# A state-space and expert network on one core: planner durations replaced, and the scan of a unit split into four scans with given first states

## The chip, the cores and the metric

The kernel runs on one core of one Trainium2 chip, as one launch. The metric is the device time of an execution in microseconds; the median of the runs is compared. TensorE (PE), VectorE (DVE), ScalarE (ACT), GpSimd (POOL) and SyncE (SP, here the queue that issues transfers) run side by side, each through its own queue in order, and wait for each other on semaphores.

## The reference, cut to what matters

A picture x of 4 batches, 256 channels and 64 x 64 places is read as 4 sequences of 4096 tokens. Layer 0 is a selective state-space mixer (512 inner channels, 16 states a channel) between projections and gates. Layer 1 is a second state-space mixer with 8 heads, and then a feed-forward layer that sends every token to one of 8 experts. The change touches the recurrence of layer 0:

```python
def step(h, inp):
    dt_l, B_l, C_l, x_l = inp
    dA = jnp.exp(dt_l[..., None] * A)
    h = dA * h + (dt_l * x_l)[..., None] * B_l[:, None, :]
    y = jnp.einsum('bdn,bn->bd', h, C_l)
    return (h, y)
h0 = jnp.zeros((Bb, D_INNER, D_STATE), t.dtype)
_, ys = jax.lax.scan(step, h0, xs)
```

So for each batch, channel d and state n there is one first-order recurrence over 4096 tokens, which starts from zero. Its input is u B with u = dt x.

## The kernel before

**Stages.** `mixers` computes both mixers and the routing, `experts` the feed-forward layer in blocks of 256 tokens, `turn` the transposed output. Only `mixers` is touched.

**Chunks.** `mixers` goes through 64 chunks of T = 256 tokens, 16 for each batch. A chunk passes the steps front0, mid0, scan, tail0 and front1, and two chunks later ssd and back1, so that the steps of several chunks lie in flight together.

**Units of the scan.** In `scan`, a chunk's 512 channels with 16 states are 16 units (j, f), j over 4 blocks of channels, f over 4 sets of states. In a unit the 128 partitions hold 32 channels with 4 states each, and 4 groups q of such channels lie behind each other, 256 tokens each: tiles of 128 x 4 x 256. A unit has these operations:

- da = exp(dt A): 4 ScalarE activations, one for each q, with the column `neg_a0[:, j * SQ + q, f : f + 1]` as scale (dt4 is dt, spread over the partitions).
- ub = u4 * B: one VectorE product of 128 x 1024 into the PSUM tile `ub`, of which there is one.
- h: one VectorE `tensor_tensor_scan` over the 1024 elements as one line, from 0.0.
- hlast: a ScalarE copy of the last column of each group, the first state of the next chunk.
- p = h * C: a GpSimd product of 128 x 1024, then 8 TensorE matmuls that add p up into `py`.

Because one scan runs over four groups, a group's first decay has to be zero, or the state of the group ahead would run into it. The three da buffers (`decay_tile`) therefore get a zero in column 0 once, ahead of the stage, and the activations write columns 1 to 255. What the true first decay would bring, exp(dt A) at the first token times hlast of the chunk before, is computed apart as `e0` (once for each j: product on GpSimd, exponential on ScalarE, product on GpSimd) and added to column 0 of ub, the VectorE addition ub<-ub,e of 128 x 4. Chunks that begin a batch have no such correction: 60 chunks of 64 have it, that is 960 units of 1024.

**The order of the work.** Nothing in the stage is issued directly. `Plan` (r in the code) notes every operation with an engine, a duration, its operands and a slot, and `order` then plays it through: an event loop in which each free engine takes, of the operations that are ready and have room for their tiles, the one with the lowest slot. The order of the starts in this play is the order in which `issue` puts the instructions into the engines' queues (L378 is the line that issues, so all of them carry it in the profile). What enters:

- The durations come from formulas in `mm`, `transpose`, `act`, `copy`, `acts`, `dve`, `gps`, `dma` and `scatter`.
- `SIGNAL`, 0.15 us, is added between an operation and a user on another engine; on the same engine nothing is.
- `slot`: a chunk's number times 16, plus the step's place, plus a due-time shift from the table `SHIFT`, looked up by how many calls of `at` the chunk has made. For most calls of `scan` the shift is -2.2, for most others -0.3.
- `port`: GpSimd operations and VectorE operations with two operands in SBUF are not played at the same time. The scan, with ub in PSUM, is not such an operation.
- `ride`: p waits, up to `PATIENCE` = 4 us, until a scan has just begun, and gets a dependency on the VectorE instruction ahead of that scan, so that it runs beside the scan.

Of the kernel before, what the change touches and what calls it, by code (L numbers as in the profile page):

```python
# [20 lines left out]
P = 128  # L21
T = 256
# [24 lines left out]
SHIFT = {  # L47
    1: -2.3, 4: 1.4, 5: 0.2, 6: -1.3, 7: -0.3, 8: -0.3, 9: -0.3, 10: -0.3, 11: -0.3, 12: -0.3, 14: -0.3, 15: -0.3,
    16: -0.3, 17: -0.3, 18: -0.3, 19: -0.3, 20: -0.3, 21: -0.3, 22: -0.3, 23: -0.3, 24: -0.3, 25: -0.3, 26: -3.3,
    27: -2.2, 28: 0.2, 29: -0.1, 30: -2.2, 31: -2.2, 32: -2.2, 33: -2.2, 34: -2.2, 35: -2.2, 36: -2.2, 37: 1.2,  # L50
    38: 0.5, 39: -2.2, 40: -2.1, 41: -2.2, 42: -2.7, 43: -2.2, 44: -2.2, 45: -6.0, 46: -2.2, 47: -2.2, 48: -2.2,
    49: -2.2, 50: -2.2, 51: -2.2, 52: -9.4, 53: -2.2, 54: -1.4, 55: -2.2, 56: -2.2, 57: -2.2, 58: -2.2, 59: -2.2,
    60: -4.7, 61: -2.2, 62: -2.2, 63: -2.2, 64: -2.2, 65: -2.2, 66: -2.2, 67: -2.7, 68: -2.2, 69: -2.2, 70: -2.2,
    71: -0.1, 72: -2.2, 73: -2.2, 74: -2.2, 75: -5.9, 76: -4.8, 77: -2.2, 78: -2.2, 79: -2.7, 80: -2.2, 81: -2.2,
    82: -2.2, 83: -2.2, 84: -2.2, 85: -5.2, 86: -2.2, 87: -2.2, 88: -2.2, 89: -2.2, 90: -2.2, 91: -1.4, 92: -2.2,
    93: -2.2, 94: -2.2, 95: -2.7, 96: -2.2, 97: -2.2, 98: -2.2, 99: -2.2, 100: -2.2, 101: -2.2, 102: -2.2,
    103: -2.2, 104: -2.2, 105: -2.2, 106: -2.3, 107: -4.0, 108: -2.0, 109: -2.2, 110: -2.2, 111: -2.2, 112: -2.2,
    113: -1.8, 114: -1.3, 115: 0.9, 116: -0.3, 117: 1.8, 118: -0.3, 119: 0.1, 120: -0.3, 121: -0.3, 123: -0.3,
    124: -0.3, 125: -0.3, 126: 0.6, 127: -1.2, 128: -0.3, 129: -0.3, 130: 0.3, 131: 0.4, 132: -1.4, 133: -0.3,
    134: -0.3, 135: -0.3, 136: 1.6, 137: -0.3, 140: 0.6,  # L60
}
# [88 lines left out]
class Plan:  # L150
# [6 lines left out]
    SIGNAL = 0.15  # L157
# [61 lines left out]
    def mm(self, out, left, right, **kw):  # L219
        rows, n = out.shape[0], self.width(right)  # L220
        w = max(0.24, n / 550) if rows > 64 else max(0.16, n / 900) if rows > 32 else max(0.15, n / 1500)
        self.note("PE", w, self.nc.tensor.matmul, (out, left, right), kw, (out,), (left, right), join=out.root)

    def transpose(self, out, src, ident):
        w = 0.08 + 0.1 * src.shape[0] / P
        self.note("PE", w, self.nc.tensor.transpose, (out, src, ident), {}, (out,), (src,), join=out.root)

    def act(self, out, src, func, **kw):
        w = 0.2 + self.width(out) / 1200
        self.note("ACT", w, self.nc.scalar.activation, (out, src, func), kw, (out,), (src, *kw.values()))  # L230

    def copy(self, out, src):
        self.note("ACT", 0.2 + self.width(out) / 1200, self.nc.scalar.copy, (out, src), {}, (out,), (src,))
# [7 lines left out]
    def dve(self, name, *args, **kw):  # L241
        out, *rest = (*args, *kw.values())
        tensors = [a for a in rest if isinstance(a, Part) or hasattr(a, "ap")]
        n = max(self.width(a) for a in (out, *tensors))
        port = len([a for a in tensors if self.on_sbuf(a) and self.width(a) > 1]) > 1
        if name == "tensor_tensor_scan":
            n, port = 2 * n, False
        op = self.note("DVE", 0.14 + n / 960, getattr(self.nc.vector, name), args, kw, (out,), rest, port=port)
        op.scan = name == "tensor_tensor_scan"
        if op.scan:  # L250
            self.scans.append(op)

# [3 lines left out]
    def gps(self, name, *args, ride=False, **kw):  # L256
        w = 0.3 + self.width(args[0]) * 2.02e-3
        f = getattr(self.nc.gpsimd, name)
        self.note("POOL", w, f, args, kw, (args[0],), args[1:], port=True, ride=ride)
# [7 lines left out]
    def scatter(self, out, rows, src, bound):  # L267


        def f(out, rows, src):  # L270
            return self.nc.gpsimd.indirect_dma_start(
                out=out,
                out_offset=bass.IndirectOffsetOnAxis(ap=rows, axis=0),
                in_=src,
                in_offset=None,
                bounds_check=bound,
                oob_is_err=False,
            )

        self.note("POOL", 1.8, f, (out, rows, src), {}, (out,), (rows, src), lag=4.0)  # L280
# [3 lines left out]
    def order(self):  # L284
# [16 lines left out]
        for op in self.ops:  # L301
            if not op.missing:
                heappush(waiting[op.engine], (0.0, op.seq, op))
        done = 0
        scan = before = last = shared = None

        def room(op, now):
            for root in op.roots:
                if not root.begun:
                    ring, queue = rings.setdefault(root.ring, []), queues[root.ring]  # L310
                    ring[:] = [o for o in ring if o.left or o.until + self.SIGNAL > now]
# [6 lines left out]
        while done < len(self.ops):  # L318
# [6 lines left out]
            for e in engines:  # L325
# [3 lines left out]
                if free[e] > now:  # L329
                    continue  # L330
# [17 lines left out]
                heappush(events, free[e])  # L348
                if op.port:
                    port[e] = free[e]  # L350
# [7 lines left out]
                for root in op.roots:  # L358
                    root.left -= 1
                    root.until = max(root.until, op.end)  # L360
                    if not root.left:
                        heappush(events, root.until + self.SIGNAL)
                for u in op.users:
                    u.missing -= 1
                    late = op.end if u.engine == e and not op.lag else op.end + self.SIGNAL
# [23 lines left out]
def tile_conv_attn_hybrid(ctx: ExitStack, tc: tile.TileContext, a: dict, out: bass.AP, cap: int, st: int):  # L389
# [41 lines left out]
    def mixers(es):  # L431
# [220 lines left out]
        def silus(*tiles, gates=0):  # L652
# [5 lines left out]
            r.acts(sum(0.2 + Plan.width(t) / 1200 for t in tiles) / len(calls) + 2.6 / len(calls), calls)  # L658
# [162 lines left out]
        da_bufs = []  # L821
        for i in range(3):
            t = wp.tile([P, SQ, T], F32, name=f"da{i}", tag=f"da{i}")
            nc.gpsimd.memset(t[:, :, 0:1], 0.0)
            da_bufs.append(t)
        turn = iter(range(10**9))

        def decay_tile():
            return r.tile(lambda: da_bufs[next(turn) % len(da_bufs)], [P, SQ, T], "da", len(da_bufs))

        def scan(k_):
# [10 lines left out]
            for j in range(KD):  # L842
# [17 lines left out]
                k_.at(j * SQ - 1)  # L860
                if later:

                    e0 = work([P, SQ, SQ], "e0", 2)
                    r.gps("tensor_tensor", e0, neg_a0[:, sl], dt4[:, :, 0:1].to_broadcast([P, SQ, SQ]), ALU.mult)
                    r.act(e0, e0, AF.Exp)
                    r.gps("tensor_tensor", e0, e0, k_.prev.hlast[:, sl], ALU.mult)
                for f in range(SQ):
# [3 lines left out]
                    da = decay_tile()  # L871
                    for q in range(SQ):
                        r.act(da[:, q, 1:], dt4[:, q, 1:], AF.Exp, scale=neg_a0[:, j * SQ + q, f : f + 1])
# [3 lines left out]
                    if later:  # L877
                        r.tt(ub[:, :, 0], ub[:, :, 0], e0[:, :, f], ALU.add)
                    h = work([P, SQ, T], "h", 3)
                    r.dve("tensor_tensor_scan", h.flat(), da.flat(), ub.flat(), 0.0, ALU.mult, ALU.add)  # L880
# [652 lines left out]
```

## Time and profile before

| | us |
|---|---|
| median of 3 runs | 6952.74 |
| lowest, highest | 6948.43, 6954.37 |
| the profiled execution, its own time | 6966.12 |
| its span, first to last instruction | 6964.3 |
| first scan to last scan | about 110 to 5727 |
| experts | about 5727 to 6870 |
| output | about 6870 to 6964 |

The granted TensorE clock was 0.906 on average. In the profile's rows, out<-in names the tiles of the program; sizes are partitions x elements. A row of a group gives the busy time of all its instructions, the mean of one in ns, and the idle time of the engine just before them with what ended it. A row of the timeline gives start and duration in us. Durations of two instructions in a row on VectorE can overlap, since the next may start before the one ahead has left the pipeline; where this matters, the distance between two starts is the measure.

### The profile page before, as it was taken

The numbers are of one execution on the slowest core, as the hardware profiler recorded it, in microseconds if no ns is written. First come the engines' busy times: TensorE is split into PE (matmuls) and PEld (weight loads), VectorE is DVE, ScalarE is ACT, GpSimd is POOL, SyncE is SP. The second block draws the span as 40 slices with busy tenths as digits, with TensorE's granted clock in tenths as the row PEclk, the third lists the DMA queues.
The fourth block names the chain that finished last, engine by engine and source line by source line (L and its number), as shares of the span: only waits on it lengthen the run. The fifth ranks groups of instructions, "written<-read, shape, count | busy, mean of one in ns | idle before, by whom it ended". The sixth has DMA issues, their size and how long they took to land. (4 is left out here: it accounts for less than half of the span.)

```text
span 6964.3 us, 114017 instructions
## 1 busy us (share of the span) xinstructions
PE 6084.7 (87%) x37672; PEld 4128.5 (59%) x37672; DVE 5670.3 (81%) x7646; ACT 4892.5 (70%) x12007; POOL 3431.0 (49%) x2632
## 2 busy tenths in 40 slices
PE   5788888888888888888888888888888877999996
PEld 3455555555555555555555555555555546888886
DVE  4899999999999999999999999999999983434443
ACT  4778888888887778788887777878777863333332
POOL 3455555555555555555555555555555552333331
PEclk7899999999888988998898888989888888999998
DMA  6966667666666666666666666666666633555556
GB/s 178 255 172 178 181 178 182 178 178 178 178 177 173 174 172 176 174 176 171 174 178 177 175 178 176 179 177 176 171 175 176 174 106 132 189 194 197 193 191 238
DMA packets 1125137, 1245.56 MB, mean 179 GB/s; under 512 B 111888, under 2 KB 1093652, under 8 KB 1115330
## 3 DMA queue, kind: packets, MB, share of 16 engines
q1 hardware_dynamic: 1083458, 1008.76, 54.9%
q0 software_dynamic: 30000, 210.98, 8.5%
q10 hardware_dynamic: 11088, 18.53, 0.7%
q8 instruction: 299, 4.90, 0.3%
q14 instruction: 292, 2.39, 0.1%
HBM read 919.92 MB, written 311.63 MB: 177 GB/s over the span
## 5 line engine op out<-in xcount | busy, mean ns | idle before, releaser
L378 POOL TENSOR_TENSOR p<-h,bc 128x1024 f32<-128x1024 f32 x1024 | 2420.7, 2364 | 1980.3 <-DVE ub L378 1371.8
L378 DVE TENSOR_TENSOR_SCAN h<-da,ub 128x1024 f32<-128x1024 f32 x1024 | 2341.8, 2287 | 190.5 <-ACT da L378 69.1
L378 ACT ACTIVATE da<-dt,w_m_Alog 128x255 f32<-128x255 f32 x4096 | 1791.1, 500 | 26.1 <-DVE h L378 17.6
L378 DVE TENSOR_TENSOR ub<-u,bc 128x1024 f32<-128x1024 f32 x1024 | 1370.2, 1338 | 23.9 <-DMA dt<-dt_d 11.5
L378 PE MATMUL py<-p,sum 128*32 128x256 f32 x8192 | 719.0, 434 | 255.2 <-POOL p L378 242.9
L378 PE MATMUL b<-t,w_W_in 128*128 128x256 f32 x2304 | 640.2, 424 | 17.6 <-DVE res L378 10.5
L378 ACT COPY hlast<-h 128x4 f32<-128x4 f32 x1024 | 198.7, 194 | 598.7 <-DVE h L378 596.8
L378 PEld LDWEIGHTS py<-p,sum 128*32 128x32 f32 x8192 | 182.0, 114 | 693.9 <-POOL p L378 399.4
L378 PEld LDWEIGHTS b<-t,w_W_in 128*128 128x128 f32 x2304 | 458.7, 208 | 163.8 <-issue 44.2
L378 PE MATMUL a<-t,w_m_in_w 128*128 128x256 f32 x2048 | 549.8, 422 | 3.5 <-DVE t L378 3.5
L1381 PE MATMUL ph<-xt,w 128*128 128x256 f32 x2272 | 517.1, 381 | 11.5 <-DMA w<-in_w_exp_dram,w_at 6.4
L378 PEld LDWEIGHTS a<-t,w_m_in_w 128*128 128x128 f32 x2048 | 415.9, 211 | 149.5 <-issue 61.0
L1392 PE MATMUL po<-w,hid 128*128 128x256 f32 x2272 | 502.0, 379 | 0.0
L1381 PEld LDWEIGHTS ph<-xt,w 128*128 128x128 f32 x2272 | 427.3, 191 | 70.4 <-ACT hid L1383 7.3
L1392 PEld LDWEIGHTS po<-w,hid 128*128 128x128 f32 x2272 | 431.7, 190 | 58.7
L378 PE MATMUL a<-raw,taps_m 128*32 128x256 f32 x2048 | 211.3, 492 | 234.1 <-DMA raw<-raw_d 169.9
L378 PE MATMUL c<-cum,after 128*128 128x512 f32 x512 | 325.7, 724 | 96.8 <-DVE ex L378 89.9
L1358 DVE CAST number<-rows 128x2 uint32<-128x2 f32 x71 | 12.0, 170 | 476.1 <-DMA tok_d<-fixed,number 461.4
L1356 ACT ACTIVATE tn<-rows 128x256 f32<-128x256 f32 x142 | 82.5, 597 | 414.0 <-DMA rows<-buf_d,row_at 413.5
L1404 POOL DMA_INDIRECT tok_d<-fixed,number x142 | 145.9, 1028 | 390.0 <-DVE fixed L1402 307.6
L378 ACT ACTIVATE cum<-upto,da 128x128 f32<-128x128 f32 x1024 | 337.4, 396 | 0.0
L378 ACT ACT_TABLE_LOAD x256 | 328.4, 1283 | 4.5
(237 smaller groups left out, 11087.4 us busy)
## 6 DMA issues: line engine op xcount, KB each, us to landing
raw<-raw_d SPq DMA_DIRECT2D x2048, 128.0 KB
dt<-dt_d SPq DMA_DIRECT2D x1024, 128.0 KB
u<-u_d SPq DMA_DIRECT2D x1024, 128.0 KB
raw_d<-raw SPq DMA_DIRECT2D x128, 518.0 KB
gx_d<-pre SPq DMA_DIRECT2D x64, 1024.0 KB
bc<-bc_d SPq DMA_DIRECT2D x1024, 64.0 KB
gx<-gx_d SPq DMA_DIRECT2D x256, 256.0 KB
dt_d<-mid SPq DMA_DIRECT2D x64, 512.0 KB
```

What stands on the lines that cost most here:

```text
L378: op.issued = f(*map(placed, args), **{k: placed(v) for k, v in kw.items()})
L1356: act(tn[:, j], rows[:, j, TOK:], AF.Identity, scale=rows[:, j, 1:2], bias=rows[:, j, 2:3])
L1358: nc.vector.tensor_copy(number, rows[:, :, 3])
L1381: mm(ph, w1[:, k, f * P : (f + 1) * P], xt[:, k], start=k == 0, stop=k == KC - 1)
L1392: mm(po[:, j], hid[:, f, j * P : (j + 1) * P], w2[:, f], start=f == 0, stop=f == KF - 1)
L1404: nc.gpsimd.indirect_dma_start(out=tok_d, out_offset=bass.IndirectOffsetOnAxis(ap=number[:, j : j + 1], axis=0), in_=fixed[:, j], in_offse ...
```

## The change

It has two parts.

**The planner.** The table `SHIFT` is emptied, so every step has its plain slot. The durations of `mm`, `transpose`, `act`, `copy`, `acts`, `dve`, `gps` and `scatter` get new constants; an activation is charged 0.09 us more for each operand that is a column. `SIGNAL` becomes a value for each engine (0.12 to 0.21), and `BEHIND` is added between dependent operations of the same engine (0.13 for VectorE, 0.14 for ScalarE, 0.13 for GpSimd, none for TensorE). After a transfer 0.06 is added. In the play SP takes no further transfer while eight (`LANES`) are in flight.

**The scan.** A unit's scan becomes four of 256 elements, noted as one operation of the plan by the new `scans_of`, each with a first state: the column of the chunk before's hlast, or 0.0 in a chunk that begins a batch. The activations write all 256 columns of da, which becomes an ordinary tile with three buffers. The chain e0 (two GpSimd products and one exponential for each j), the addition to ub, the three da buffers and their memsets go.

```diff
--- before.py
+++ after.py
@@ -44,21 +44,7 @@
 TAIL, SSD, BACK = 18, 29, 37
 AHEAD = 4
 
-SHIFT = {
-    1: -2.3, 4: 1.4, 5: 0.2, 6: -1.3, 7: -0.3, 8: -0.3, 9: -0.3, 10: -0.3, 11: -0.3, 12: -0.3, 14: -0.3, 15: -0.3,
...
-}
+SHIFT = {}
 TOK = 4
 ROW = TOK + C
 
@@ -154,7 +140,9 @@
 
 
 
-    SIGNAL = 0.15
+    SIGNAL = {"DVE": 0.13, "ACT": 0.19, "PE": 0.21, "POOL": 0.12}
+    BEHIND = {"DVE": 0.13, "ACT": 0.14, "PE": 0.0, "POOL": 0.13}
+    LANES = 8
     SPARE = {}
     PATIENCE = 4.0
 
@@ -218,19 +206,20 @@
 
     def mm(self, out, left, right, **kw):
         rows, n = out.shape[0], self.width(right)
-        w = max(0.24, n / 550) if rows > 64 else max(0.16, n / 900) if rows > 32 else max(0.15, n / 1500)
+        w = max(0.224, n / 592) if rows > 64 else max(0.12, n / 1100) if rows > 32 else max(0.15, n / 1500)
         self.note("PE", w, self.nc.tensor.matmul, (out, left, right), kw, (out,), (left, right), join=out.root)
 
     def transpose(self, out, src, ident):
-        w = 0.08 + 0.1 * src.shape[0] / P
+        w = 0.11 if src.shape[0] > 64 else 0.2
         self.note("PE", w, self.nc.tensor.transpose, (out, src, ident), {}, (out,), (src,), join=out.root)
 
     def act(self, out, src, func, **kw):
-        w = 0.2 + self.width(out) / 1200
+        aps = sum(isinstance(v, Part) or hasattr(v, "ap") for v in kw.values())
+        w = 0.06 + self.width(out) / 1130 + 0.09 * aps
         self.note("ACT", w, self.nc.scalar.activation, (out, src, func), kw, (out,), (src, *kw.values()))
 
     def copy(self, out, src):
-        self.note("ACT", 0.2 + self.width(out) / 1200, self.nc.scalar.copy, (out, src), {}, (out,), (src,))
+        self.note("ACT", 0.05 + self.width(out) / 1200, self.nc.scalar.copy, (out, src), {}, (out,), (src,))
 
     def acts(self, weight, calls):
 
@@ -245,16 +234,26 @@
         port = len([a for a in tensors if self.on_sbuf(a) and self.width(a) > 1]) > 1
         if name == "tensor_tensor_scan":
             n, port = 2 * n, False
-        op = self.note("DVE", 0.14 + n / 960, getattr(self.nc.vector, name), args, kw, (out,), rest, port=port)
+        op = self.note("DVE", (0.06 if n > 4 else 0.14) + n / 960, getattr(self.nc.vector, name), args, kw, (out,), rest, port=port)
         op.scan = name == "tensor_tensor_scan"
         if op.scan:
             self.scans.append(op)
 
+    def scans_of(self, out, a, b, starts):
+
+        key, f = object(), self.nc.vector.tensor_tensor_scan
+        for i, start in enumerate(starts):
+            args = (out[:, i], a[:, i], b[:, i], start, ALU.mult, ALU.add)
+            w = 0.07 + self.width(out[:, i]) / 480
+            op = self.note("DVE", w, f, args, {}, (out[:, i],), (a[:, i], b[:, i], start), join=key)
+        op.scan = True
+        self.scans.append(op)
+
     def tt(self, out, a, b, op):
         self.dve("tensor_tensor", out, a, b, op)
 
     def gps(self, name, *args, ride=False, **kw):
-        w = 0.3 + self.width(args[0]) * 2.02e-3
+        w = 0.15 + self.width(args[0]) * 2.1e-3
         f = getattr(self.nc.gpsimd, name)
         self.note("POOL", w, f, args, kw, (args[0],), args[1:], port=True, ride=ride)
 
@@ -277,7 +276,7 @@
                 oob_is_err=False,
             )
 
-        self.note("POOL", 1.8, f, (out, rows, src), {}, (out,), (rows, src), lag=4.0)
+        self.note("POOL", 1.4, f, (out, rows, src), {}, (out,), (rows, src), lag=4.0)
 
 
 
@@ -301,6 +300,7 @@
         for op in self.ops:
             if not op.missing:
                 heappush(waiting[op.engine], (0.0, op.seq, op))
+        lanes, landings = ("SP",), []
         done = 0
         scan = before = last = shared = None
 
@@ -308,7 +308,7 @@
             for root in op.roots:
                 if not root.begun:
                     ring, queue = rings.setdefault(root.ring, []), queues[root.ring]
-                    ring[:] = [o for o in ring if o.left or o.until + self.SIGNAL > now]
+                    ring[:] = [o for o in ring if o.left or o.until > now]
                     while queue[-1].begun:
                         queue.pop()
                     if len(ring) + (queue[-1] is not root) * self.SPARE.get(root.ring, root.depth) >= root.depth:
@@ -326,7 +326,7 @@
                 while waiting[e] and waiting[e][0][0] <= now:
                     _, _, op = heappop(waiting[e])
                     insort(could[e], (op.slot, op.seq, op))
-                if free[e] > now:
+                if free[e] > now or e in lanes and len(landings) >= self.LANES and landings[-self.LANES] > now:
                     continue
                 for i, (_, _, op) in enumerate(could[e]):
 
@@ -346,6 +346,9 @@
                 op.start, op.end = now, now + op.weight + op.lag
                 free[e] = now + op.weight
                 heappush(events, free[e])
+                if e in lanes:
+                    landings.append(op.end)
+                    heappush(events, op.end)
                 if op.port:
                     port[e] = free[e]
                 if e == "DVE":
@@ -357,12 +360,12 @@
                     op.behind = before if scan and now - scan.start < 0.2 else shared
                 for root in op.roots:
                     root.left -= 1
-                    root.until = max(root.until, op.end)
+                    root.until = max(root.until, op.end + (0.06 if op.lag else self.SIGNAL[e]))
                     if not root.left:
-                        heappush(events, root.until + self.SIGNAL)
+                        heappush(events, root.until)
                 for u in op.users:
                     u.missing -= 1
-                    late = op.end if u.engine == e and not op.lag else op.end + self.SIGNAL
+                    late = op.end + (0.06 if op.lag else (self.BEHIND if u.engine == e else self.SIGNAL)[e])
                     u.ready = max(u.ready, late)
                     if u.ride and not u.missing:
                         heappush(events, u.ready + self.PATIENCE)
@@ -655,7 +658,7 @@
 
             calls += [(half_tanh, (t[:, :KC],), t[:, :KC], t[:, :KC]) for t in tiles[:gates]]
             calls.append((nc.scalar.preload_act_table_set, (SETS,), None, None))
-            r.acts(sum(0.2 + Plan.width(t) / 1200 for t in tiles) / len(calls) + 2.6 / len(calls), calls)
+            r.acts(sum(0.06 + Plan.width(t) / 1130 for t in tiles) / len(calls) + 2.6 / len(calls), calls)
 
         def inv_sqrt(dst, src, eps, scale=1.0):
 
@@ -818,16 +821,6 @@
 
 
 
-        da_bufs = []
-        for i in range(3):
-            t = wp.tile([P, SQ, T], F32, name=f"da{i}", tag=f"da{i}")
-            nc.gpsimd.memset(t[:, :, 0:1], 0.0)
-            da_bufs.append(t)
-        turn = iter(range(10**9))
-
-        def decay_tile():
-            return r.tile(lambda: da_bufs[next(turn) % len(da_bufs)], [P, SQ, T], "da", len(da_bufs))
-
         def scan(k_):
             later = k_.c > 0
             k_.hlast = work([P, NG, SQ], "hlast", 2)
@@ -857,27 +850,18 @@
                     for s in range(2):
                         r.dma("SP", gx[:, s], k_.gx_d[s * KD + j : s * KD + j + 2].rearrange("j p l -> p j l"))
                 sl = slice(j * SQ, (j + 1) * SQ)
-                k_.at(j * SQ - 1)
-                if later:
-
-                    e0 = work([P, SQ, SQ], "e0", 2)
-                    r.gps("tensor_tensor", e0, neg_a0[:, sl], dt4[:, :, 0:1].to_broadcast([P, SQ, SQ]), ALU.mult)
-                    r.act(e0, e0, AF.Exp)
-                    r.gps("tensor_tensor", e0, e0, k_.prev.hlast[:, sl], ALU.mult)
                 for f in range(SQ):
                     u = j * SQ + f
                     bc = bc4[f]
                     k_.at(u - 1)
-                    da = decay_tile()
+                    da = work([P, SQ, T], "da", 3)
                     for q in range(SQ):
-                        r.act(da[:, q, 1:], dt4[:, q, 1:], AF.Exp, scale=neg_a0[:, j * SQ + q, f : f + 1])
+                        r.act(da[:, q], dt4[:, q], AF.Exp, scale=neg_a0[:, j * SQ + q, f : f + 1])
                     k_.at(u)
                     ub = bank_u(SQ, T)
                     r.tt(ub, u4, bc[:, 0, None, :].to_broadcast([P, SQ, T]), ALU.mult)
-                    if later:
-                        r.tt(ub[:, :, 0], ub[:, :, 0], e0[:, :, f], ALU.add)
                     h = work([P, SQ, T], "h", 3)
-                    r.dve("tensor_tensor_scan", h.flat(), da.flat(), ub.flat(), 0.0, ALU.mult, ALU.add)
+                    r.scans_of(h, da, ub, [k_.prev.hlast[:, j * SQ + q, f : f + 1] if later else 0.0 for q in range(SQ)])
                     k_.at(u + 1)
                     r.copy(k_.hlast[:, sl, f], h[:, :, T - 1])
```

## The prediction

> **What bounds the kernel now.** I read the page's busy shares first, then busy time by stage, the groups of one stage by shape, a few microseconds of VectorE's timeline, and its waits. The page:
>
> ```profile
> PE 6084.7 (87%) x37672; PEld 4128.5 (59%) x37672; DVE 5670.3 (81%) x7646; ACT 4892.5 (70%) x12007; POOL 3431.0 (49%) x2632
> ```
>
> The stages, columns as in the header:
>
> ```profile
> core 0: us, PE busy (x) PEld busy (x) DVE busy (x) ACT busy (x) POOL busy (x), PEclk, DMA share, GB/s
> ...
> 110.00:5727.00 5617.00, 4886.75 (x31925) 3099.77 (x31925) 5174.04 (x6686) 4481.31 (x11126) 3037.20 (x2198) 0.90 0.67 178
> 5727.00:6870.00 1143.00, 1089.51 (x5265) 943.62 (x5265) 458.15 (x896) 357.82 (x781) 371.59 (x368) 0.97 0.49 174
> ```
>
> On the page TensorE leads with 87%, but that is an average over two stages. From 110 to 5727 us (first scan to last, the only part that the change edits) VectorE is busy 92%, TensorE 87%, ScalarE 80%; the experts behind it are TensorE's and stay as they are. In the middle of that stage (2000 to 4000 us), by shape:
>
> ```profile
> L378 POOL TENSOR_TENSOR p<-h,bc 128x1024 f32<-128x1024 f32 x363 | 857.4, 2362 | 686.8 <-DVE ub L378 479.2 <-PE a L378 70.7 <-DMA gx<-gx_d 47.1
> L378 DVE TENSOR_TENSOR_SCAN h<-da,ub 128x1024 f32<-128x1024 f32 x363 | 830.2, 2287 | 72.3 <-ACT da L378 29.6 <-POOL p L378 2.2 <-DVE ub L378 0.5
> L378 DVE TENSOR_TENSOR ub<-u,bc 128x1024 f32<-128x1024 f32 x362 | 491.6, 1358 | 2.9 <-DMA xtail<-in_x_dram 0.3
> L378 DVE TENSOR_TENSOR ub<-ub,e 128x4 f32<-128x4 f32 x346 | 58.4, 169 | 11.9
> L378 POOL TENSOR_TENSOR e<-e,hlast 128x16 f32<-128x16 f32 x86 | 46.7, 543 | 93.7 <-DMA raw<-raw_d 55.5 <-ACT e L378 33.0 <-DVE g L378 4.9
> L378 POOL TENSOR_TENSOR e<-w_m_Alog,dt 128x16 f32<-128x16 f32 x87 | 40.6, 467 | 7.5 <-DVE ub L378 4.1 <-DMA dt<-dt_d 2.0 <-PE c L378 1.4
> ```
>
> Scan and product ub are two thirds of VectorE's work. The idle 72.3 us before the scans is only half explained by named waits; the rest is the hand-over from one VectorE instruction to the next, which the timeline shows (start, duration):
>
> ```profile
> 3005.10 1.23 DVE L378 TENSOR_TENSOR ub<-u,bc 128x1024 f32<-128x1024 f32 x1
> 3006.36 0.17 DVE L378 TENSOR_TENSOR ub<-ub,e 128x4 f32<-128x4 f32 x1
> 3006.66 2.29 DVE L378 TENSOR_TENSOR_SCAN h<-da,ub 128x1024 f32<-128x1024 f32 x1
> 3008.86 0.39 DVE L378 TENSOR_TENSOR state<-state,c 128x256 f32<-128x256 f32 x1
> 3009.17 0.68 DVE L378 SCALAR_TENSOR_TENSOR z<-z,b 128x512 f32<-128x512 f32 x1
> ...
> 3038.71 0.46 DVE L378 SCALAR_TENSOR_TENSOR row<-c,rr,res 128x264 f32<-128x264 f32 x1
> 3039.09 1.22 DVE L378 TENSOR_TENSOR mid<-mid,mid 128x1024 f32<-128x1024 f32 x1
> ```
>
> Count from start to start. An instruction that depends on the one before waits for its end (ub, then the correction 1.26 later, then the scan 0.30 later); one that doesn't depend starts some 0.08 us before that end (2.20 after a scan that lasts 2.29). VectorE's waits for others in the same 2000 us are small:
>
> ```profile
> DVE h L378 <- ACT da L378: 29.6, 29, 1.4
> DVE g L378 <- PE py L378: 17.8, 18, 2.0
> DVE xdt L378 <- PE c L378: 17.5, 18, 1.6
> DVE shift L378 <- ACT scale L378: 16.4, 22, 1.0
> ```
>
> All rows of such waits add up over the whole stage to about 255 us, 4.5%. So VectorE's own pitch sets the time, and each step is priced as VectorE time, medians over the stage's 1024 units (960 of them in chunks after a batch's first).
>
> **The change part by part.**
>
> *One scan becomes four.* A scan of 1024 takes 2204 ns to the next independent start: 2133 at two cycles an element, 71 beside. Four of 256 are 4 x (533 + 71) = 2417, so +213 x 1024 = +218 us.
>
> *Each start read from memory.* The trace has no scan with such an operand. Nearest rows: row<-c,rr,res has a column as scalar and 264 elements (275 ns), and the next independent start comes after 404, 129 over; state<-state,c of 256 without one is 45 over, z<-z,b of 512 with a constant 64 over. In the set-up, w_m_in_w<-w_m_in_w,w_ln_g is 156 over its 533 and, in the experts, fixed<-y with constants 75 over its 267. A column costs 65 to 85 ns more. Upper bound 85 x 3840 = 326 us; lower bound 0, if the read hides under the scan in front. A gain is excluded, it is an extra read. I take 65, from the row that reads PSUM too, as the scan does: +250 us. The wait that comes with the column is for hlast of the chunk before, copied a chunk (some 88 us) earlier; nothing queues behind it. The 64 first chunks start from a constant.
>
> A rule speaks against these two edits. The Trainium skill, VectorE: DVE Perf Modes, section "The DRAIN you can't avoid", says that the next operation doesn't start until the pipeline is empty, and its rules for authors tell to keep the count of operations low. By that each scan would cost its full 687 ns (2287 less 768 elements at two cycles), four 2748, +461 x 1024 = +472 us instead of +218. The trace has independent starts 83 ns before the end, and the same section allows an earlier start to an operation that isn't held; I keep +218.
>
> *The correction of u B goes.* 960 x 301 ns from its start to the scan's: -289 us.
>
> *ub is followed by the scan at once.* The 51 such pairs of the trace (mostly the first chunks) have a median of 1356 ns against 1262 to the correction: +94. With another operation between, ub takes 1136, so -126. The new planner charges 0.13 us between dependent VectorE operations (the old charged nothing) and will put something between where anything is ready. VectorE has about four other operations per unit; I take 65%: 960 x (0.35 x 94 - 0.65 x 126) = -47, and -9 in the first chunks: -56 us. If nothing fills: +90.
>
> *The e0 chain goes:* 480 POOL products and 240 ScalarE exponentials. On POOL 220 us in all, with their own idle (93.7 us before the second in 2000 us); p is queued behind them, and the tile's view has p wait 233.9 us for e in this window. POOL is idle 46% and ScalarE 20%, so this is worth nothing directly. What it does is free p's start: ub and a few others run about 120 us longer than their medians over the stage, nearly all beside a p that started late and missed the scan. With POOL freer and the four scans longer than p (2.4 to 2.7 against 2.36 us) I take a third back: -40 us.
>
> *The order.* SHIFT goes; durations, hand-overs and a bound of eight SP transfers in flight come in. Nothing is computed differently and no transfer is added or removed, but every instruction, SP's and POOL's queues included, can change its place. What it can win is the 255 us of waits and hand-overs in chains of small operations (some 13 a chunk at 0.20 instead of 0.09 us, about 90 us). The old constants err most on ScalarE: 0.2 + n/1200 sums to 4510 us where pitches sum to about 4160, so the old order was built around a ScalarE that is fuller than the real one. The new sum is about 3790, too low. The new VectorE sum leaves out the columns, so the real VectorE will be later than planned and its suppliers early: I take half of the waits, -125, and half of the small chains with some scan-to-ub hand-overs, -55. Bounds: -255 from no waits at all, +130 from half as many again, if SHIFT's placing was worth more than the new constants.
>
> *Nothing:* decays of 256 instead of 255 (4096 elements at 0.8 ns, 3 us on ScalarE, under its idle 20%; if that were gone, 3 us); da from the work pool with the same three buffers, three memsets less before the stage.
>
> Sum: 218 + 250 - 289 - 56 - 40 - 125 - 55 = -97 us. Made against the profiled execution (6966.1 us, of which the span is 6964.3) that is 6869; that execution lies 13 us over the median 6952.74 of the runs, so 6856.
>
> **The rivals.**
>
> *Column reads are hidden.* The sum is without the 250: -347, so 6606, say 6620. For: a scan runs 533 ns, time enough to fetch the next one's column. Against: the column of w_ln_g wasn't hidden behind an equal instruction just before it.
>
> *The four starts aren't bought back (slower).* Place: VectorE, each unit. Price: 218 + 250 - 289 = +179, with ub's direct hand-over +90: +269. With 65% filled, and waits and collisions as now, it is +123, 7076; with none filled 7222. So it decides where order and collisions give back less than 123 us. For: the waits are only 4.5%, and an order can win no more than they hold. Against: the new plan knows the hand-over. I take 7080.
>
> *The order is worse without SHIFT.* Waits rise by 130, no small chain gains: about +213, 7166. For: 141 due times shifted one by one go. Against: VectorE was late against the old plan too, and now more.
>
> *The order doesn't change what VectorE does:* possible where queues stay as they are; included in the slower case.
>
> **How the numbers follow.** About 0.2% (14 us) is what a measurement of this kernel can tell from no change. Likeliest case 0.53, 6856, own range 6740 to 6950 (faster 0.49, same 0.03, slower 0.01); hidden columns 0.27, 6620, all faster; not bought back 0.14 (same 0.01, slower 0.13); worse order 0.06 (same 0.01, slower 0.05). Faster 0.76, same 0.05, slower 0.19. The range 6600 to 7080 takes in most of the hidden-column case and the lower half of the slower one, and leaves out about 0.2.
>
> **What would show it.** After: 4096 scans of 256, from start to start about 670 ns with a column and 604 in first chunks (all 604: the first rival). No ub<-ub,e, no e rows. ub to the next start nearer 1136 than 1356 in more than half of the units. VectorE's named waits for ScalarE and TensorE half of 255 us, ub's mean nearer 1300 than the page's 1338. I'd be wrong if the waits grew or another engine took the bound: ScalarE over 90% or p's waits for something other than ub.

## The result, and the profile after

The changed kernel takes 6843.9 us (median of 4 runs, 6837.9 to 6847.1) against 6953.3 us for the kernel before (4 runs, the three of the table above and one more), 109 us less: ratio 0.9843, 95% interval 0.9826 to 0.9860. Forecast was 6856 us. The profiled execution took 6837.9 us with a span of 6836.2. That span is 128 us shorter than the one before, more than the medians differ, since the profiled execution of before lay 13 us over its median and this one 6 us under. The page's busy row, and the stages by time (columns as in the prediction); the stage from the first scan to the last now ends at 5606 us, and the experts and the output behind it last about as long as before (1230 us against 1237):

```profile
PE 5991.5 (88%) x37672; PEld 4083.5 (60%) x37672; DVE 5756.3 (84%) x9758; ACT 4880.7 (71%) x11767; POOL 3154.1 (46%) x2149
```

```profile
110.00:5606.00 5496.00, 4793.90 (x31921) 3054.14 (x31925) 5260.59 (x8801) 4469.70 (x10887) 2758.54 (x1716) 0.93 0.71 182
5606.00:6836.00 1230.00, 1137.12 (x5529) 985.37 (x5524) 480.36 (x927) 376.12 (x813) 374.17 (x369) 0.96 0.53 189
```

VectorE is busier than before, 87 us more in a stage that is 121 us shorter (96% of it against 92%). The groups from 2000 to 4000 us, by shape:

```profile
L381 DVE TENSOR_TENSOR_SCAN h<-da,hlast,ub 128x256 f32<-128x256 f32 x1418 | 941.7, 726 | 16.2 <-DVE dest L381 0.4
L381 POOL TENSOR_TENSOR p<-h,bc 128x1024 f32<-128x1024 f32 x371 | 874.3, 2357 | 834.6 <-DVE ub L381 114.2 <-DVE xdt L381 109.8 <-DVE decay L381 92.6
L381 DVE TENSOR_TENSOR ub<-u,bc 128x1024 f32<-128x1024 f32 x370 | 496.8, 1343 | 1.7
L381 DVE TENSOR_TENSOR_SCAN h<-da,ub 128x256 f32<-128x256 f32 x64 | 38.7, 665 | 0.7
```

The row ub<-ub,e and both e rows are gone. The idle time before the scans is down from 72.3 to 16.2 us. But ub is nearly as slow as it was, 1343 ns on average against 1358. A scan with a column lasts 726 ns on average, one with a constant 665. VectorE's timeline (start, duration; x4 are the four scans):

```profile
2999.87 1.23 DVE L381 TENSOR_TENSOR ub<-u,bc 128x1024 f32<-128x1024 f32 x1
3001.02 0.17 DVE L381 TENSOR_TENSOR ex<-hot,base_slot 128x16 f32<-128x16 f32 x1
3001.21 2.66 DVE L381 TENSOR_TENSOR_SCAN h<-da,hlast,ub 128x256 f32<-128x256 f32 x4
3003.78 0.14 DVE L381 TENSOR_REDUCE red<-ex 128x2 f32<-128x16 f32 x1
...
3016.40 1.25 DVE L381 TENSOR_TENSOR ub<-u,bc 128x1024 f32<-128x1024 f32 x1
3017.79 2.66 DVE L381 TENSOR_TENSOR_SCAN h<-da,hlast,ub 128x256 f32<-128x256 f32 x4
```

Between ub and its scan there is now mostly an operation of another chain (ex, above), in 73% of the units over the whole stage against 16% before; where there is none, as in the last two lines, the scan comes 1.39 us after ub's start. VectorE's two largest waits for others from 2000 to 4000 us:

```profile
DVE stats L381 <- PE b L381: 34.1, 18, 3.4
DVE row L381 <- issue: 19.3, 23, 1.2
```

For the accounts below I added up VectorE's whole stage in each trace: the distance from each start to the next, put to the instruction that started, except idle times of 160 ns and more, which stand apart as waits. "Correction" is the addition ub<-ub,e, "small" are other instructions shorter than 230 ns. The rows below "after" are the experiments of the next section. All in us:

| | stage | scans | ub | correction | small | rest | waits |
|---|---|---|---|---|---|---|---|
| before | 5618 | 2284 | 1400 | 269 | 246 | 1165 | 255 |
| after | 5497 | 2658 | 1345 | 0 | 195 | 1125 | 175 |
| planner_only | 5438 | 2295 | 1249 | 174 | 190 | 1268 | 263 |
| scans_only | 5482 | 2647 | 1375 | 0 | 255 | 1141 | 64 |
| no_correction | 5313 | 2279 | 1425 | 0 | 254 | 1180 | 175 |
| constant_start | 5344 | 2436 | 1375 | 0 | 194 | 1135 | 204 |
| no_handover | 5686 | 2652 | 1426 | 0 | 260 | 1186 | 162 |
| with_shift | 5486 | 2637 | 1223 | 0 | 191 | 1226 | 211 |
| scatter_behind_p | 5459 | 2658 | 1238 | 0 | 202 | 1130 | 231 |
| scans_handover | 5438 | 2635 | 1292 | 0 | 214 | 1117 | 180 |

From before to after: scans +374, correction -269, waits -80, ub -55, small -52, rest -40, together -122.

The granted clock of TensorE in this stage rises from 0.90 to 0.93 as well, so a faster TensorE is a rival explanation of the shorter waits. Over the runs the waits do not follow the clock: they are 263 us at 0.93 (planner_only), 162 at 0.89 (no_handover), 64 at 0.94 (scans_only) and 175 at 0.95 (no_correction). A part of it can't be excluded, since no run holds the clock apart from the order.

### The profile page after: what moved, and what is told of

It reads as the page before. It is cut to its first block, busy times and chain, and to the rows that moved or that the text cites. A ratio compares the mean times of both kernels' runs of the same rounds, so it can differ in the third digit from the quotient of the medians.

```text
span 6836.2 us, 114750 instructions
## 1 busy us (share of the span) xinstructions
PE 5991.5 (88%) x37672; PEld 4083.5 (60%) x37672; DVE 5756.3 (84%) x9758; ACT 4880.7 (71%) x11767; POOL 3154.1 (46%) x2149
## 5 line engine op out<-in xcount | busy, mean ns | idle before, releaser
L381 DVE TENSOR_TENSOR_SCAN h<-da,hlast,ub 128x256 f32<-128x256 f32 x3840 | 2550.2, 726 | 46.1 <-ACT da L381 2.3
L381 ACT ACTIVATE da<-dt,w_m_Alog 128x256 f32<-128x256 f32 x4096 | 1836.0, 501 | 2.8 <-DMA dt<-dt_d 2.3
L381 DVE TENSOR_TENSOR ub<-u,bc 128x1024 f32<-128x1024 f32 x1024 | 1372.0, 1340 | 16.7 <-DMA u<-u_d 11.4
L381 PE MATMUL py<-p,sum 128*32 128x256 f32 x8192 | 680.6, 405 | 372.3 <-POOL p L381 361.6
L381 PE MATMUL b<-t,w_W_in 128*128 128x256 f32 x2304 | 602.2, 404 | 56.4 <-ACT raw L381 37.6
L381 PEld LDWEIGHTS b<-t,w_W_in 128*128 128x128 f32 x2304 | 431.4, 196 | 226.5 <-ACT raw L381 95.6
L381 PE MATMUL a<-t,w_m_in_w 128*128 128x256 f32 x2048 | 499.1, 393 | 4.1 <-DVE t L381 4.1
L381 PEld LDWEIGHTS a<-t,w_m_in_w 128*128 128x128 f32 x2048 | 378.7, 192 | 129.6 <-issue 50.6
L1367 ACT ACTIVATE hid<-ph,w 128x256 f32<-128x256 f32 x426 | 188.5, 467 | 164.0 <-PE ph L1365 163.4
```

Source lines behind the costliest of these rows:

```text
L381: op.issued = f(*map(placed, args), **{k: placed(v) for k, v in kw.items()})
L1367: act(hid[:, f], ph, AF.Relu, bias=b1[:, f : f + 1])
```

## The experiments

Ratios are to the kernel before on the same chip, with their 95% intervals; the medians of that kernel lie between 6942 and 6968 us from chip to chip. Diffs are cut to the lines that matter, with "..." where lines are left out.

**planner_only**: the planner as changed, the scan as before.

```diff
--- after
...
+                    if later:
+                        r.tt(ub[:, :, 0], ub[:, :, 0], e0[:, :, f], ALU.add)
...
-                    r.scans_of(h, da, ub, [k_.prev.hlast[:, j * SQ + q, f : f + 1] if later else 0.0 for q in range(SQ)])
+                    r.dve("tensor_tensor_scan", h.flat(), da.flat(), ub.flat(), 0.0, ALU.mult, ALU.add)
```

> The planner as changed (constants, hand-overs, eight transfers, no SHIFT), with the scan of before: one scan of 1024 from 0.0, the e0 chain and the correction of ub. Theory (VectorE's pitch sets the time and the order alone pays): the change's scan part costs VectorE, so this kernel is faster than the changed one. By pitches with gaps filled, a unit is 1136 + 80 to 300 + 2204 here against 1136 + 2556 there, 70 to 270 ns less, over 960 units 65 to 260 us: 6590 to 6780 us, say 6700. Rival (the gain is the scan part, which takes the correction and the e0 chain out): no faster than before, 6900 to 6960 us.

Measured 6783.5 us, 0.9764 (0.9748 to 0.9781). The upper end of what was expected is missed by 4 us, the rival by over 100: the planner alone is worth about 164 us and beats the whole change. The table says where: ub -151, correction -95 and small -56, because gaps are filled and p seldom runs beside a ub. The rest grows by 103, of which 57 are the product decay<-decay,gm held up beside a p, in nearly every chunk. The waits grow by 8.

**scans_only**: the four scans, the planner and SHIFT as before.

```diff
--- before
...
-                    if later:
-                        r.tt(ub[:, :, 0], ub[:, :, 0], e0[:, :, f], ALU.add)
...
-                    r.dve("tensor_tensor_scan", h.flat(), da.flat(), ub.flat(), 0.0, ALU.mult, ALU.add)
+                    r.scans_of(h, da, ub, [k_.prev.hlast[:, j * SQ + q, f : f + 1] if later else 0.0 for q in range(SQ)])
```

> The scan part as changed, with the planner of before: its constants, its SHIFT table (the calls are counted as before, so each step keeps its shift), and the four scans priced together as the one scan was, 2.273 us. Theory: VectorE pays 4 x 578 less 2204 (+111 us), 3840 columns at 61 ns (+234), ub straight to the scan (+90 less what is filled), and gains the correction (-289): slower than before by 80 to 150 us, 7030 to 7100 us. Rival (the scan part is the gain): about as fast as the changed kernel, 6830 to 6870 us.

Measured 6825.3 us, 0.9827 (0.9811 to 0.9844). My theory is refuted: the scan part alone isn't slower by 80 to 150 us, it is faster by 123, as fast as the whole change. The VectorE terms are as the theory had them (scans +363, correction -269), but the waits fall from 255 to 64, and that it didn't have. VectorE's three largest waits in the same 2000 us:

```profile
DVE gm L388 <- PE c L388: 7.1, 16, 1.6
DVE stats L388 <- PE b L388: 2.6, 3, 1.2
DVE g L388 <- PE py L388: 1.3, 2, 0.8
```

The waits of the scan for da, of g for py, of xdt and of shift, which led the list of before, are all but gone.

**constant_start**: the changed kernel with every first state 0.0; it leaves out the state that a chunk hands to the next, and keeps the order of every queue.

```diff
-                    r.scans_of(h, da, ub, [k_.prev.hlast[:, j * SQ + q, f : f + 1] if later else 0.0 for q in range(SQ)])
+                    r.scans_of(h, da, ub, [0.0] * SQ)
```

> The changed kernel with 0.0 as first state everywhere, so the state isn't carried from chunk to chunk; nothing else differs, the order neither. Theory: a scan with a column has 639 ns to the next start, with a constant 578, so 3840 x 61 = 234 us of VectorE time go, and nearly all of it shows: 6610 to 6680 us. Rival (another engine or a fixed order is nearly as late, TensorE is busy 87% and ScalarE 81%): less than half shows, 6730 to 6844 us.

Measured 6688.1 us, 0.9627 (0.9611 to 0.9644), against 0.9843 with columns: 156 us. So the column is a real cost and is paid on VectorE. From start to start, the four scans of a row take 662, 638, 638 and 638 ns with columns in the trace of the changed kernel (medians by place in the row), and 604, 578, 578 and 578 with constants, there as here. But of 222 us that the scans lose here, 153 reach the stage; ub, rest and the waits grow by 69. The time lies 8 us over the theory's range and outside the rival's.

**no_handover**: the changed kernel, planned without the 0.13 us.

```diff
-    BEHIND = {"DVE": 0.13, "ACT": 0.14, "PE": 0.0, "POOL": 0.13}
+    BEHIND = {"DVE": 0.0, "ACT": 0.14, "PE": 0.0, "POOL": 0.13}
```

> The changed kernel, planned with no hand-over time between dependent VectorE operations (0 in place of 0.13). Theory: ub is followed by its scan at once in 80% of the units or more, where in the changed kernel something lies between in 73%; each such unit loses 0.2 us, so slower by 90 to 150 us, 6930 to 7000 us. Rival (the gaps cost nothing on the whole, since the order only moves them, or the gain came from the other constants): within 30 us, 6815 to 6875 us.

Measured 7035.2 us, 1.0130 (1.0113 to 1.0147): slower than the kernel before, and by 191 us than the changed one. The share of ub with something behind it falls from 73 to 21%; ub +81, rest +61, small +66. The theory is right in direction and too low in size: it counted ub alone, and chains of small operations lose nearly as much. Without this one constant the rest of the new planner is worth nothing here; the others were not taken out one by one, but for the price of the scatter (below).

**no_correction**: the kernel before without the e0 chain and the addition; it leaves out the state that a chunk hands to the next.

```diff
-                if later:
-
-                    e0 = work([P, SQ, SQ], "e0", 2)
...
-                    if later:
-                        r.tt(ub[:, :, 0], ub[:, :, 0], e0[:, :, f], ALU.add)
```

> The kernel before, planner and SHIFT as they were, with the e0 chain and the addition to ub left out (so the state isn't carried between chunks); the scan stays one of 1024. It asks why scans_only lost 190 us of VectorE's waits. Theory A (e0 stood in the queues of GpSimd and ScalarE and made others late): besides 960 x (301 - 94) = 199 us of VectorE the waits fall too, as in scans_only: 6560 to 6680 us. Theory B (the longer scans made VectorE the late one, so its suppliers came early): VectorE is shorter here, so the waits of 255 us stay or grow: 6730 to 6830 us.

Measured 6654.3 us, 0.9587 (0.9567 to 0.9607): inside theory A's range. With the e0 chain and the addition gone the waits fall from 255 to 175 though VectorE has less to do. Why is only in part shown: in the trace of before GpSimd stood idle 93.7 us in 2000 us ahead of the second e product, with p queued behind it, which fits e0 holding up its queues. But no run takes the chain out and keeps the addition, and taking both out gave a new order. VectorE's two largest waits are now for TensorE:

```profile
DVE stats L378 <- PE b L378: 21.3, 13, 2.6
DVE gm L378 <- PE c L378: 19.4, 24, 2.6
```

The scan's wait for da, 29.6 us before, is 1.0 here. Theory B has a part too: the planner prices a unit's scan at 2.273 us here as in scans_only, and the two plans have the same order on every queue but for some 60 places of ScalarE's. So nearly all that the two traces differ by is the four starts and columns: scans +368, waits -111, ub -50, rest -39, stage +169. A longer scan on VectorE is paid back by more than half: under the same order its suppliers come early, and fewer p are still running when the next ub starts (9 ub last over 1.8 us in scans_only, 123 here).

**shift_only**: the kernel before with the table emptied.

```diff
-SHIFT = {1: -2.3, 4: 1.4, ...}
+SHIFT = {}
```

> The kernel before with the SHIFT table emptied and nothing else. Theory: the table was worth something under the old constants, so emptied it costs, and planner_only's gain is the constants' alone: 6960 to 7150 us. Rival (the table was the fault, the constants do little): 6780 to 6900 us.

Measured 6959.9 us, 1.0024 (1.0005 to 1.0044): the table was worth about 17 us. So emptying it gives planner_only none of its gain, and the rival is out.

**with_shift**: the changed kernel with the table kept.

```diff
-SHIFT = {}
+SHIFT = {1: -2.3, 4: 1.4, ...}
```

> The changed kernel with the SHIFT table of before kept (calls counted as before, so each step has its old shift). Theory: the scans' lead of two slots gives the rest room, as in scans_only, and VectorE's waits fall from 175 towards 64 us: 6720 to 6800 us. Rival (the table fits the old durations alone): 6840 to 6950 us.

Measured 6839.3 us, 0.9852 (0.9831 to 0.9873), the same as without. The theory fails: ub's collisions are gone (ub 1223 against 1345), but rest +101 and waits +36 take it back.

**scatter_price**: GpSimd's scatter planned at 1.05 us.

```diff
-        self.note("POOL", 1.4, f, (out, rows, src), {}, (out,), (rows, src), lag=4.0)
+        self.note("POOL", 1.05, f, (out, rows, src), {}, (out,), (rows, src), lag=4.0)
```

> The changed kernel with GpSimd's scatter planned at 1.05 us instead of 1.4 (its median in the trace is 1.07, its mean 1.45). In the changed kernel once a chunk a p is planned to miss the scan because the second scatter still holds GpSimd, waits out its patience and runs beside a ub, which takes up to 3.1 us instead of 1.23: 118 us in all. Theory: with the lower price p is planned beside the scan and ub's excess falls below 50 us: 6750 to 6790 us. Rival (another p a chunk misses instead, or the real scatter runs over its price): 6820 to 6860 us.

Measured 6840.3 us, 0.9849 (0.9834 to 0.9863): no difference. The excess of ub, what its instances last beyond their median of 1.23 us, is still 119 us. The collision in the trace of the changed kernel (VectorE and GpSimd):

```profile
3016.39 1.02 POOL L270 DMA_INDIRECT buf_d<-row,dest  x1 [0.15 <-issue]
...
3021.15 1.22 DVE L381 TENSOR_TENSOR decay<-decay,gm 128x1024 f32<-128x1024 f32 x1
3022.28 0.68 DVE L381 TENSOR_TENSOR xdt<-c,dt 128x512 f32<-128x512 f32 x1
3022.54 2.35 POOL L381 TENSOR_TENSOR p<-h,bc 128x1024 f32<-128x1024 f32 x1 [5.13 <-DVE decay L381]
3022.88 3.10 DVE L381 TENSOR_TENSOR ub<-u,bc 128x1024 f32<-128x1024 f32 x1
3026.09 2.66 DVE L381 TENSOR_TENSOR_SCAN h<-da,hlast,ub 128x256 f32<-128x256 f32 x4
```

DMA_INDIRECT is the scatter. It is over at 3017.4, before the scan of 3017.79, so p could have ridden that scan; but the plan made p depend on decay. In the play the scatter is taken 0.03 us before the scan and at either price is still running 0.2 us into it, when a scan no longer counts as just begun; p then goes after its patience has run out and decay is done with the port. This p holds ub for 1.87 us, and the same comes about once in nearly every chunk.

**scatter_behind_p**: no scatter while a p waits.

```diff
+                    if op.engine == "POOL" and op.lag and any(o.ride for _, _, o in could[e]):
+                        continue
```

> The changed kernel with one more rule in the planner: a scatter isn't taken while a p waits for its scan. The price had not moved the miss (scatter_price): in the play the second scatter is taken 0.03 us before the scan that p waits for, at 1.05 as at 1.4 us, and p then goes beside a ub. Theory: p takes its scan, ub's excess falls from 118 to below 40 us and the time with it: 6740 to 6790 us. Rival (VectorE's other waits, 175 us of an order that is too tight, take it up): 6810 to 6850 us.

Measured 6801.6 us, 0.9765 (0.9746 to 0.9784): 0.8% better than the change by the ratios (42 us by the medians), between both ranges. ub falls by 107 us as the theory says; the waits rise by 56 as the rival says, now for the second mixer's chain:

```profile
DVE pre L383 <- PE c L383: 22.1, 31, 1.2
DVE state L383 <- PE c L383: 17.6, 24, 1.2
DVE cdec L383 <- ACT cdec L383: 10.7, 23, 0.7
```

**true_price_scatter**: the rule of scatter_behind_p, and besides the four scans priced at their measured medians (the first of a row still 24 to 26 ns too low).

```diff
...
-            w = 0.07 + self.width(out[:, i]) / 480
+            w = (0.106 if isinstance(start, Part) else 0.045) + self.width(out[:, i]) / 480
```

> As scatter_behind_p, and the four scans planned at what the trace shows: 0.639 us each with a column and 0.578 with a constant, in place of 0.603. Theory (the waits of 175 us stand because the plan is off): VectorE's waits fall towards 100 us, 30 to 80 us faster than scatter_behind_p. Rival (a VectorE that is later than planned makes its suppliers early, so the too low price helped): same or slower by up to 60 us.

Measured 6830.9 us, 0.9806 (0.9785 to 0.9828): the rival holds. With these prices VectorE's waits are 269 us instead of 231. That fits a too low price on the engine that sets the time acting as a margin for its suppliers; the order changes too, and one run doesn't separate the two.

**scans_handover**: scans_only with the hand-over alone.

```diff
...
-                    late = op.end if u.engine == e and not op.lag else op.end + self.SIGNAL
+                    late = op.end + (0.13 if e == "DVE" else 0.0) if u.engine == e and not op.lag else op.end + self.SIGNAL
```

> scans_only (planner and SHIFT of before, the four scans) with one thing of the new planner: 0.13 us between dependent VectorE operations. Theory (the hand-over is what the new planner wins with): more than half of the ub get something between them and their scan instead of a quarter, idle time of VectorE below 160 ns falls from 134 to about 70 us, waits stay near 64: 6720 to 6780 us. Rival (what is filled there comes back as waits): 6800 to 6840 us.

Measured 6780.4 us, 0.9739 (0.9715 to 0.9762): at the edge of the theory's range, and with planner_only the fastest kernel of the study that leaves nothing out. Filled ub are 73% (25% in scans_only), ub -84, small -41. But the waits don't stay near 64, they come to 180.

**scans_handover_scatter**: scans_handover with the rule of scatter_behind_p.

```diff
...
+                    if op.engine == "POOL" and op.lag and any(o.ride for _, _, o in could[e]):
+                        continue
```

> scans_handover with the rule of scatter_behind_p: the planner and SHIFT of before, the four scans, 0.13 us between dependent VectorE operations, and no scatter taken while a p waits for its scan. Theory: ub's excess of 66 us (31 collisions over 1.5 us) falls below 30 and VectorE's waits stay near 180: 6730 to 6770 us, the fastest of all. Rival (as in scatter_behind_p, half or more comes back as waits for TensorE): 6770 to 6800 us.

Measured 6797.7 us, 0.9767 (0.9747 to 0.9786): the rival, and no gain on scans_handover. ub's excess is gone (2.6 us of 66), but VectorE has a new wait. Its waits in 2000 us, and what GpSimd does:

```profile
DVE ex L390 <- PE c L390: 80.2, 23, 5.6
```

```profile
3012.88 2.75 POOL L281 DMA_INDIRECT buf_d<-row,dest  x1 [0.16 <-DMA bc<-bc_d]
3015.65 0.22 POOL L390 TENSOR_TENSOR seen<-seen,hot 128x8 f32<-128x8 f32 x1
3017.24 2.36 POOL L390 TENSOR_TENSOR p<-h,bc 128x1024 f32<-128x1024 f32 x1 [1.37 <-DMA u<-u_d]
3019.75 1.01 POOL L281 DMA_INDIRECT buf_d<-row,dest  x1 [0.15 <-issue]
```

The scatters are put off until no p waits, and seen, a small GpSimd operation, stands behind a scatter of 2.75 us in GpSimd's queue. A matmul reads seen, and the trace puts the 80.2 us of ex to it. One stall was exchanged for another.

## Why the prediction was right, and where its steps were not

The time came within 12 us: the sum of -97 us stands against -109 by the medians and -122 in VectorE's account. The terms, and which of them hold:

- **Four starts: +218, measured +137.** The prediction gave each scan 604 ns to the next start, 533 by the planner's formula (2n/960 us, its "two cycles an element") and 71 beside it, as the long scan has. The first scan of a row has these 604 ns. But each of the three that follow a scan has 578, so the four take 2338 ns, not 2417. The 26 ns were not in the trace of before, where no scan follows another; why they go is open. The strict reading of the drain in the Trainium skill (VectorE: DVE Perf Modes, "The DRAIN you can't avoid"), by which each scan would hold VectorE for its whole duration (660 ns here), would have made it +446; it is not what the trace shows, where the next start comes 82 ns before the end.
- **Columns: +250, measured +229** (58 ns in the first scan of a row and 60 in the others, against 65 taken). Scan and column together are +366 by these medians; the whole scan row of the table rose by 374. The first rival, hidden columns, is excluded by the two distances, and constant_start shows that some 150 us of it reach the time.
- **The correction: -289**, in the table -269, without its waits.
- **ub straight to the scan: -56.** Filled are 73% against 65% taken, with 1136 and 1364 ns where 1136 and 1356 were expected. The mechanism is right, and no_handover shows that it is the 0.13 us that does it.
- **Collisions: -40 was wrong.** ub's excess is 118 us, as before (113), and its mean on the page 1340 ns, where nearer 1300 than 1338 was the sign. The new order had a place for a collision in nearly every chunk by a decision of its own, which no duration in the trace of before could tell.
- **Small chains: -55, measured -52**; the rest, for which I had nothing, gave 40 more.
- **Waits: -125, measured -80, and put to the wrong cause.** I gave them to the new order. The new planner alone leaves them at 263; it is the scan part that lowers them, to 64 under the old order. Two things were missed. The e0 chain was costed at nothing because GpSimd and ScalarE are idle for part of the time (46% and 20%); without it and its addition the waits are 80 us less, probably because it stood in their queues. And the longer scans, written down in full as VectorE's time, came back by 111 us of waits, 50 of ub and 39 of the rest.

So the split between the parts was wrong, and that the total held is in part luck: scans and columns cost 94 us less than priced and the rest gave 40 unpriced, while collisions, waits and correction gave some 100 less than forecast. By the prediction's terms the scan part without filling would have cost 179 to 269 us, to be bought back by the order; the slower case was built on that, and scans_only refutes it: in the stage, taking the chain and the addition out saves 305 us (no_correction), and four starts with columns take 169 of it back.

Each part alone is a gain, 123 and 164 us, and together they are worth 109. By the table the stage gains 136 and 180 us from the parts and 121 from both, 195 less than their sum. Of this, 95 are time of the correction, which the planner saves and the scan part takes out anyway; 121 are ub, which meets the collision in the chosen order; 103 are waits, which open again where gaps are closed (64 to 180 from scans_only to scans_handover). The rest and the small operations give 123 back. Why the new planner's orders wait more for the second mixer's chain on TensorE and ScalarE wasn't tested; the lower prices that it has for both engines are a possible cause.

The rival of a worse order without SHIFT is out: the table moves the time by 0.24% in shift_only and by nothing measurable in with_shift.

## What to carry to other kernels

Count the time of the engine that sets the pace from start to start and give the hand-over between dependent instructions a price in the scheduler; here that one constant was worth some 190 us, and the planner's other new values without it (no_handover) left the kernel 3% behind scans_only. A short helper on an engine that is often idle need not be free, since it stands in that engine's queue ahead of others: ask who is queued behind it, not only how busy the engine is. And before two edits are judged as one, run each alone: here either half was as good as the whole or better.

## What the runs showed of the hardware that was not expected

That a product on GpSimd and one on VectorE with two operands in SBUF get in each other's way was in the planner's port rule; how much was not. A GpSimd product of 2.35 us doesn't slow such a VectorE product by some share, it holds it until it is over. In the changed kernel 67 ub started while a p ran, and they ended 1.09 us after the p did (median), however much of p was left; most of them took about 3.10 us instead of 1.23. The product xdt, which has one operand in PSUM, isn't held: in planner_only 52 of them started beside a running p and lasted 692 ns, as the other 73 did.

A scan of 256 right behind another takes 578 ns from start to start, 26 less than the first of a row, and a first state from a column adds 58 to 60 ns wherever the scan stands in the row, though three of the four have more than 0.5 us of scan ahead of them.
